# Block 2 of a four-block network: weight pieces between the context's tiles, softmax shifts from the sums alone

## The chip, the cores and the metric

The kernel runs on one core of a Trainium2 chip. The metric is device time in microseconds of one execution; lower is better. The engines are named as in the profile: PE (matrix products and transposes), DVE (VectorE), ACT (ScalarE), POOL (GpSimd) and SP (which issues most DMAs). They run side by side, each through its own queue in order, and wait for one another through semaphores.

## The reference

Four transformer blocks (L0 to L3) work one after the other on `x` of shape 4x1024x288, with a context of 4x64 rows. The change is in block L2, which quantizes its attention to 8 bits with one scale per tensor. Cut to what matters:

```python
def _fake_quant(x, n_bits, always_zero=False):
    ...
    xq = jnp.clip(_ste_round(x / delta) + zp, 0.0, levels)
    return (xq - zp) * delta

def _quant_attention(x, ctx, Wq, Wk, Wv, Wo, bo):
    q, k, v = ...                       # 16 heads of 18
    q = _fake_quant(q, NBITS)
    k = _fake_quant(k, NBITS)
    v = _fake_quant(v, NBITS)
    scores = jnp.einsum('bhqd,bhkd->bhqk', q, k) * scale
    probs = jax.nn.softmax(scores, axis=-1)
    probs = _fake_quant(probs, SMBITS, always_zero=True)   # one scale: max(probs) / 255
    out = jnp.einsum('bhqk,bhkd->bhqd', probs, v)
    return out.transpose(0, 2, 1, 3).reshape(bsz, sq, D) @ Wo + bo

n1 = _ln(h, ln1_g, ln1_b)
h = h + _quant_attention(n1, n1, Wq1, Wk1, Wv1, Wo1, bo1)                       # self-attention
h = h + _quant_attention(_ln(h, ln2_g, ln2_b), encoder_hidden_states, ...)      # context
n3 = _ln(h, ln3_g, ln3_b)
a, gate = jnp.split(n3 @ Wff1 + bff1, 2, axis=-1)
h = h + a * jax.nn.gelu(gate, approximate=False) @ Wff2 + bff2
```

The scale of the probabilities is their maximum over all rows and heads. So no probability can be rounded before all of them have been seen once.

## The kernel before

A tile is 128 rows of `x`; there are 32, eight to each of the four batch entries. The 16 heads are padded from 18 to 32 columns and stand in four groups (`g`) of four heads, so that a group fills 128 partitions after a transpose. A framework plans the order within each engine's queue from the order in which the code is traced, priorities and modelled times; `tc.issue_after(i)` puts what it encloses behind instruction `i` on `i`'s engine. In `fq_tail`, SP alone keeps the order of the code. A tile of a pool that takes over memory waits for the last reader of what lay there.

Block L2 runs through these stages:

- The projections write `raw`, queries, keys and values of all tiles, to DRAM, and their extremes give the scales `q` (`super().global_params`, with one reduction over the partitions on POOL).
- **First pass** (`fq_passes`, first half). `fetch` brings columns of `raw` into one of three buffers `in`; `fq_levels` and `place` round them and put them into padded tiles `pads`; `operands` or `both` transposes these on PE and ACT copies them to `qk` (L3180). For batch entry 0 the keys are made by DVE, and the queries by the generator `first_queries` on POOL. Then for each group, tile and pair of heads: scores on PE (`scores_pair`, L3842), exponentials with row sums on ACT (L3244), and the largest exponential of each row on DVE (L3251). While one batch entry is scored, `levels` prepares the next on POOL.
- **Hand-over.** `largest` turns sums and maxima into the largest probability, `prob_params` makes the scale `pd` of it over all partitions by way of PE. Each row then gets a shift, minus the logarithm of sum times `pd`: `y = sums * pd`, its Ln and one correction step (`log_shifts`), split into three bf16 parts. `add_shift` puts the parts into three of the unused rows of each head in `qk`'s queries (D to D+2, through `spad` on POOL, a transpose and an addition on DVE); the keys hold ones in these rows, so that the score's product adds the shift.
- **Second pass** (`attend_levels`). For half a batch entry (512 queries), group and tile of keys `kt`: scores from `kz`, the keys of a group spread with zeros by SP's DMAs (`spread`); exponentials (L3891) that come out as levels, rounding on DVE (L3897) and products with the values (L3865). `beside_half` does one step of other work at each `kt`: it adds the shifts of the next half, and projects and normalizes the last one.
- **Context** (`fq_tail`). `largest(t)` makes a tile's query levels (L819, L820, L3545), transposes them (L3551), writes them to `qb` in DRAM (L3555), scores them (L3558) and takes maxima (L3565); POOL does every second tile from the fourth on. `total(n, qT)` sums the exponentials of four tiles (L3576 to L3607). After the first four, `load_halves` loads the feed-forward weight `w1`: a large load and six pieces of 384 columns through two buffers `w3`, each cast and subtracted on DVE (L2661, L2662), and then `w2` and the biases. Afterwards shifts are made on POOL (`parts_of`) from the logarithm of the sums alone, and the scale's logarithm enters the exponential as a bias `lp[:, 2:3]`.

Of the kernel before, what the change touches and what calls it, by code (L numbers as in the profile page):

```python
# [37 lines left out]
P = 128  # L38
# [1142 lines left out]
class Fast(Net):  # L1181
# [65 lines left out]
    def prob_params(self, pool, r, name):  # L1247

        nc = self.nc
        s = pool.tile([P, 1], F32, name=f"{name}s")  # L1250
        nc.vector.tensor_reduce(s, r, AX.X, ALU.max)
        d = pool.tile([P, 1], F32, name=f"{name}d")
        nc.vector.tensor_scalar(
            d, self.largest_of(pool, s, name), 1.0 / 255.0, None, ALU.mult
        )
        return d
# [1393 lines left out]
    def load_halves(self, pool, scratch, w, n, name, step):  # L2650
# [5 lines left out]
        for c0 in range(0, n, step):  # L2656
            m = min(step, n - c0)
            cols = slice(c0, c0 + m)
            y = scratch.tile([P, step], F32, tag="w3", name="w3", bufs=2)[:, :m]
            nc.sync.dma_start(y, w[2 * P :, cols])  # L2660
            nc.vector.tensor_copy(c[:, cols], y)  # L2661
            nc.vector.tensor_tensor(  # L2662
                c[64:, cols], y[64:], c[64:, cols].bitcast(F32), ALU.subtract
            )
        return t, c
# [248 lines left out]
    def fq_attn(self, w, ctxT, beside):  # L2914
# [10 lines left out]
        with ExitStack() as es:  # L2925
# [145 lines left out]
            self.watch_range(-0.5, 255.5, q["zp"], "zext")  # L3071

# [7 lines left out]
    def fq_passes(self, w, q, step, raw, rawq, qmx, qmn, side, aside):  # L3080

        tc, nc = self.tc, self.nc
        with ExitStack() as es:
# [7 lines left out]
            nc.gpsimd.memset(v[:, :, C:], 0.0)  # L3091

            kzs = [gp.tile([P, 2, S], BF16, name="kz0")]
# [12 lines left out]
            top = tp.tile([P, NT, H], F32, name="top")  # L3106
            sums = tp.tile([P, NT, H], F32, name="sums")
            r = tp.tile([P, NT, H], F32, name="rs")
            tmx = tp.tile([P, B], F32, name="tmx")
            with (  # L3110
# [7 lines left out]
                for pd in pads:  # L3118
                    nc.gpsimd.memset(pd, 0.0)
                    nc.gpsimd.memset(pd[:, 1, :, D : D + 3], 1.0)  # L3120

                def fetch(b, n, j0, m):

                    y = ld.tile([P, 3 * C], F32, tag="in", name="in")
# [4 lines left out]
                def place(b, n, j, y, eng):  # L3129
# [6 lines left out]
                    eng.tensor_scalar(dst, src, q["top"][:, n : n + 1], None, ALU.min)  # L3136

                def first_queries():

                    for j0 in range(0, NTB, 3):  # L3140
# [65 lines left out]

                fq0 = first_queries()
                next(fq0)
                for j0 in range(0, NTB, 3):
                    m = min(3, NTB - j0)  # L3210
                    y = fetch(0, 1, j0, m)
# [5 lines left out]
                operands(0, 0, 0, 1)  # L3217
                nc.gpsimd.memset(kzs[0], 0.0)
                for sp in spads:
                    nc.gpsimd.memset(sp, 0.0)  # L3220
                spare = iter(())
                for b in range(B):
                    ahead = levels(b + 1) if b + 1 < B else first_values()
                    for g in range(NG):
                        for qt in range(NTB):
# [3 lines left out]
                            with tc.issue_after(self.last) if n or b else nullcontext():  # L3229
                                if b == 0 and g == 0 and qt + 1 < NTB:  # L3230
# [8 lines left out]
                            for pr in range(2):  # L3239
# [3 lines left out]
                                for j, sc in enumerate(scs):  # L3243
                                    nc.scalar.activation(  # L3244
# [5 lines left out]
                                    )  # L3250
                                nc.vector.tensor_reduce(top[:, t, h0 : h0 + 2], e, AX.X, ALU.max)  # L3251
                            if n in (2, 3):
                                next(spare, None)
                    if b + 1 < B:
# [6 lines left out]
                    spare = largest(b)  # L3261
                for _ in spare:
                    pass
            es.enter_context(self.psum("f1o"))
            pd = self.prob_params(gp, tmx, "pd")
            rt = gp.tile([P, 1], F32, name="rstep")
            nc.vector.reciprocal(rt, step)
            parts = gp.tile([P, 3, NT * H], BF16, name="parts")
            flat = lambda ap: ap.rearrange("p t h -> p (t h)")
            y = flat(sums)  # L3270
            z, u = (tp.tile([P, NT * H], F32, name=k) for k in ("lsz", "lsu"))
            nc.vector.tensor_scalar(y, y, pd, None, ALU.mult)
            nc.scalar.activation(z, y, AF.Ln)

            def log_shifts(c0, c1):

                yc, zc, uc = (ap[:, c0:c1] for ap in (y, z, u))
                nc.scalar.activation(uc, zc, AF.Exp, scale=-1.0)
                nc.vector.tensor_tensor(uc, uc, yc, ALU.mult)
                nc.vector.tensor_scalar(uc, uc, -1.0, 1.0, ALU.mult, ALU.add)  # L3280
                nc.vector.tensor_tensor(uc, uc, zc, ALU.subtract)
                nc.vector.tensor_scalar(uc, uc, rt, None, ALU.mult)
                for k in range(3):
                    nc.vector.tensor_copy(parts[:, k, c0:c1], uc)
                    if k < 2:
                        nc.vector.tensor_tensor(uc, uc, parts[:, k, c0:c1], ALU.subtract)

            def shifts(b, hf):
                for j in range(hf * 4, hf * 4 + 4):
                    t = b * NTB + j  # L3290
                    self.add_shift(
                        qk[:, b, 0, :, j * P : (j + 1) * P], spads[j % 2], parts, t
                    )
                    yield

            with tops:
                log_shifts(0, NTB * H)
                for _ in shifts(0, 0):
                    pass
# [706 lines left out]
```

## Time and profile before

| what | value |
|---|---|
| median of 3 runs | 4738.31 us (4733.14 to 4739.08) |
| the profiled execution | 4733.92 us, its span 4732.1 us |
| busy PE, DVE, ACT, POOL | 4196.1, 3077.9, 2999.1, 1193.8 us |
| mean granted PE clock | 0.88 |
| first pass, first to last reduction of L3251 | 1734.06 to 2304.84 us |
| second pass, exponentials L3891 | 2323.22 to 2824.25 us |
| context, first level to `pds` | 2858.25 to 2981.60 us |

The times of the stages are microseconds from the start of the span. A matmul's end is modelled, so PE's busy time is no measure of its rate. The chain of waits that the profile follows back from the end names, in each stretch, what the following work waited for.

### The profile page before, as it was taken

To read this page: it belongs to the slowest core of one execution; us is meant where nothing else is said; L and a number is where in the kernel's file an instruction comes from. 1 tells how busy PE (TensorE), PEld (TensorE's weight loads), DVE (VectorE), ACT (ScalarE), POOL (GpSimd) and SP (SyncE) were. 2 spreads that over 40 slices of the span, in tenths; PEclk is the share of its full clock that TensorE was granted. 3 is DMA by queue.
4 is the path that set the end of the run, shared out by engine and by line. 5 is a ranking of instruction groups with operands and counts; after the bars stand their busy time and mean duration, and the time that the engine had idled before them with its cause. 6 is when DMAs were issued, how large, how long until landed. Compare 5 with 4: busy or idle time off the path is not lost. (4 is left out here: it accounts for less than half of the span.)

```text
span 4732.1 us, 62855 instructions
## 1 busy us (share of the span) xinstructions
PE 4196.1 (89%) x22841; PEld 1741.1 (37%) x22841; DVE 3077.9 (65%) x6914; ACT 2999.1 (63%) x4277; POOL 1193.8 (25%) x1797
## 2 busy tenths in 40 slices
PE   4999998889988889999789986899998999998887
PEld 2223323455566531111123333455552233223444
DVE  8355445786644779999888986544346446446886
ACT  2776776566753259999799973322215776775665
POOL 2001001333210567440013343210101000002453
PEclk9999999889999875555589997899998999998898
DMA  3000002110000321000001014001001000001000
GB/s 88 2 6 22 9 11 54 56 42 6 13 13 17 113 92 42 27 18 0 14 21 29 26 29 144 21 21 19 0 19 26 2 10 26 7 12 39 15 18 19
DMA packets 138592, 135.92 MB, mean 29 GB/s; under 512 B 69404, under 2 KB 116124, under 8 KB 136736
## 3 DMA queue, kind: packets, MB, share of 16 engines
q1 hardware_dynamic: 137072, 128.13, 9.2%
q0 software_dynamic: 1200, 3.69, 0.4%
q8 instruction: 181, 2.97, 0.3%
q14 instruction: 139, 1.14, 0.1%
HBM read 79.92 MB, written 43.47 MB: 26 GB/s over the span
## 5 line engine op out<-in xcount | busy, mean ns | idle before, releaser
L2196 ACT ACTIVATE e<-ps 128x1024 f32<-128x1024 f32 x1024 | 992.6, 1021 | 412.0 <-PE ps L2186 404.6
L2186 PE MATMUL ps<-qT,kT 32*128 32x512 f32 x4096 | 624.3, 647 | 2.0 <-DVE sext L2108 2.0
L3251 DVE TENSOR_REDUCE top<-e 128x2 f32<-128x2048 f32 x256 | 563.5, 2273 | 15.4 <-ACT e L3244 15.2
L2142 PE MATMUL ps<-e,v 128*32 128x512 f32 x4096 | 553.9, 612 | 9.0 <-DVE oT L2153 9.0
L3842 PE MATMUL ps<-qk 32*128 32x512 bf16 x1024 | 500.7, 604 | 40.3 <-ACT e L3244 38.6
L3244 ACT ACTIVATE e<-ps 128x1024 f32<-128x1024 f32 x512 | 521.6, 1190 | 6.6 <-PE ps L3842 3.1
L3891 ACT ACTIVATE e<-ps 128x1024 f32<-128x1024 f32 x512 | 477.1, 1080 | 33.3 <-PE ps L3882 18.5
L3897 DVE TENSOR_SCALAR eb<-e 128x2048 bf16<-128x2048 f32 x256 | 323.8, 1270 | 48.4 <-ACT e L3891 47.3
L1921 POOL TENSOR_TENSOR x<-x,y 128x288 f32<-128x288 f32 x188 | 149.1, 805 | 812.2 <-DVE y L1919 484.8
L2693 PE MATMUL psf<-hT,w 128*128 128x512 f32 x576 | 271.9, 594 | 0.7 <-ACT hT L2684 0.6
L2186 PEld LDWEIGHTS ps<-qT,kT 32*128 32x128 f32 x4096 | 184.8, 185 | 202.1 <-issue 130.3
L3882 PE MATMUL ps<-qk,kz 64*128 64x512 bf16 x1024 | 216.7, 423 | 32.3 <-ACT e L3891 27.4
L2142 PEld LDWEIGHTS ps<-e,v 128*32 128x32 f32 x4096 | 81.3, 108 | 402.7 <-issue 345.0
L3842 PEld LDWEIGHTS <-qk 32*128 32x128 bf16 x1024 | 53.1, 99 | 465.6 <-issue 464.6
L3758 ACT ACTIVATE gl<-psf,bf 128x512 f32<-128x512 f32 x72 | 49.3, 685 | 243.6 <-PE psf L2694 235.0
L2038 POOL TENSOR_TENSOR v<-y,wv1b 128x288 f32<-128x288 f32 x64 | 51.0, 802 | 565.1 <-DVE y L2035 565.1
L3244 ACT ACTIVATION_READ_ACCUMULATOR e<-ps 128x1 f32 x512 | 192.1, 375 | 0.0
L1535 POOL TENSOR_TENSOR h<-h,g 128x288 f32<-128x288 f32 x108 | 88.0, 815 | 355.5 <-ACT h L1532 355.5
L279 PEld LDWEIGHTS <-qT 98*128 98x128 bf16 (+2 forms) x1344 | 130.1, 103 | 127.4 <-ACT qT L1437 38.9
L2153 DVE COPY oT<-ps 128x512 f32<-128x512 f32 x64 | 44.1, 689 | 202.0 <-PE ps L2142 202.0
L3762 DVE SCALAR_TENSOR_TENSOR u<-psf,bf,gl 128x512 f32<-128x512 f32 x72 | 53.6, 748 | 153.0 <-PE psf L2694 152.8
L3773 PE MATMUL psf<-w,u 128*128 128x288 f32 x576 | 147.0, 410 | 0.0
(579 smaller groups left out, 7970.4 us busy)
## 6 DMA issues: line engine op xcount, KB each, us to landing
raw<-y SPq DMA_DIRECT2D x32, 432.0 KB
in<-raw SPq DMA_DIRECT2D x30, 432.0 KB
kz<-qk SPq DMA_DIRECT2D x128, 64.0 KB
wn<-in_L_wfc SPq DMA_DIRECT2D x12, 432.0 KB
x<-in_x SPq DMA_DIRECT2D x4, 1152.0 KB
vvo<-vt SPq DMA_DIRECT2D x16, 288.0 KB
vo<-vvo SPq DMA_DIRECT2D x4, 1152.0 KB
qn<-rawq SPq DMA_DIRECT2D x4, 1152.0 KB
```

Source lines behind the costliest of these rows:

```text
L1921: eng.tensor_tensor(self.x[:, t, :], self.x[:, t, :], y, ALU.add)
L2142: nc.tensor.matmul(acc[i * HP : (i + 1) * HP, :], lhsT=st["v"][:, kt, h * (D + 1) : h * (D + 1) + HP], rhs=es_[i // 2][:, i % 2, :], start ...
L2186: nc.tensor.matmul(pss[i // 2][:, i % 2, :], lhsT=self.row_tile(kT, i)[:, kt * P : (kt + 1) * P], rhs=self.row_tile(qT, i)[:, qh * 512 : ( ...
L2196: nc.scalar.activation(e, ps, AF.Exp, scale=SCALE)
L2693: nc.tensor.matmul(o, lhsT=a[:, c, :], rhs=b[:, c, :], start=(c == 0), stop=False)
L3244: nc.scalar.activation(e[:, j, :].rearrange("p (a n) -> p a n", a=2), sc, AF.Exp, scale=rstep, accum_out=sums[:, t, h0 + j : h0 + j + 1],)
L3251: nc.vector.tensor_reduce(top[:, t, h0 : h0 + 2], e, AX.X, ALU.max)
L3773: nc.tensor.matmul(ps[:, :C], lhsT=us[f][:, j * P : (j + 1) * P], rhs=w2[:, f, :], start=(f == 0), stop=(f == nf - 1),)
L3842: self.last = self.nc.tensor.matmul(ps[:, c, :], lhsT=self.row_tile(qT, i)[:, g, qt * P : (qt + 1) * P], rhs=self.row_tile(kT, i)[:, g, c ...
L3882: nc.tensor.matmul(pss[i][:, n, :], lhsT=kz[rows, i, kt * P : (kt + 1) * P], rhs=qT[rows, g, qh * 512 : (qh + 1) * 512], start=True, stop= ...
L3891: nc.scalar.activation(e[:, 2 * n : 2 * n + 2, :], ps, AF.Exp, scale=step)
L3897: nc.vector.tensor_scalar(eb, e, MAGIC, MAGIC, ALU.add, ALU.subtract)
```

## The change

Five things change in L2:

- Query tile 0 is fetched alone and made by DVE ahead of the keys, and the last two keys are fetched into a buffer of the exponentials. The transposes of query tile 1 come after the first pair of heads. The memsets of `v`, `kzs` and `spads` move from ahead of the pass to its tile 8, on POOL; range checks move behind the start.
- The shifts are made from the sums alone, on POOL, in the manner of the context stage (`log_parts`). For the first half of batch entry 0 they don't hold the scale; for all other rows the scale's part `lp[:, 2:3]` is added before the split.
- For that first half the scale's part enters as a bias of the exponential in group 0, and for groups 1 to 3 through three more rows (D+3 to D+5, six rows of ones in the keys), which one addition fills (`lps`).
- In the second pass's first half `beside_half` does that addition and the scaling of `wo`, and starts the shifts of the next half ten steps later.
- In the context stage DVE makes the levels of all tiles, and the six pieces of `w1` are loaded one per tile by a generator, after `w2` and the biases have been issued.

The diff, cut to its core:

```diff
-    def load_halves(self, pool, scratch, w, n, name, step):
+    def halves_pieces(self, pool, scratch, w, n, name, step):
 ...
+        def pieces():
+            for c0 in range(0, n, step):
 ...
+                nc.sync.dma_start(y, w[2 * P :, cols])
+                nc.vector.tensor_copy(c[:, cols], y)
+                nc.vector.tensor_tensor(
+                    c[64:, cols], y[64:], c[64:, cols].bitcast(F32), ALU.subtract
+                )
+                yield
+
+        return (t, c), pieces()
 ...
+            def log_parts(lz, lu, c0, c1, one):
+
+                yc, zc, uc = (a[:, c0:c1] for a in (flat(sums), lz, lu))
+                eng = nc.gpsimd
+                eng.tensor_tensor(uc, uc, yc, ALU.mult)
+                eng.tensor_scalar(uc, uc, -1.0, one, ALU.mult, ALU.add)
+                eng.tensor_tensor(uc, uc, zc, ALU.subtract)
+                eng.tensor_scalar(uc, uc, rt, None, ALU.mult)
+                for k in range(3):
+                    i = eng.tensor_copy(parts[:, k, c0:c1], uc)
+                    if k < 2:
+                        eng.tensor_tensor(uc, uc, parts[:, k, c0:c1], ALU.subtract)
+                return i.ins
 ...
-                    nc.gpsimd.memset(pd[:, 1, :, D : D + 3], 1.0)
+                    nc.gpsimd.memset(pd[:, 1, :, D : D + 6], 1.0)
 ...
-                fq0 = first_queries()
-                next(fq0)
+                y = fetch(0, 0, 0, 1)
+                self.fq_levels(y[:, 0, :], q, 0)
+                place(0, 0, 0, y[:, 0, :], nc.vector)
+                operands(0, 0, 0, 1)
+                fq0 = first_queries()
                 for j0 in range(0, NTB, 3):
                     m = min(3, NTB - j0)
-                    y = fetch(0, 1, j0, m)
+                    y = None
+                    if j0 == 6:
+                        y = ep.tile([P, 2, S], F32, tag="e", name="e").rearrange("p a n -> p (a n)")
+                    y = fetch(0, 1, j0, m, y)
 ...
-                operands(0, 0, 0, 1)
-                nc.gpsimd.memset(kzs[0], 0.0)
-                for sp in spads:
-                    nc.gpsimd.memset(sp, 0.0)
+                next(fq0)
+                self.watch_range(-0.5, 255.5, q["zp"], "zext")
 ...
+                                if b == 0 and n == 0 and pr == 0:
+                                    operands(0, 0, 1, 1)
 ...
+                            if b == 0 and n == NTB:
+                                with tc.issue_after(self.placed):
+                                    nc.gpsimd.memset(v[:, :, C:], 0.0)
+                                    for t in (*kzs, *spads):
+                                        nc.gpsimd.memset(t, 0.0)
 ...
+                lz, lu = (
+                    ld.tile([P, 3 * C], F32, tag="in", name="in")[:, : NT * H] for _ in range(2)
+                )
+                with tc.issue_after(ended):
+                    nc.scalar.activation(lz, flat(sums), AF.Ln)
+                    ended = nc.scalar.activation(lu, lz, AF.Exp, scale=-1.0).ins
+                with tc.issue_after(ended):
+                    nc.scalar.activation(lp[:, 0:1], rt, AF.Ln)
+                log_parts(lz, lu, 0, NTB * H // 2, 1.0)
                 for _ in spare:
                     pass
+                pd = self.prob_params(gp, tmx, "pd")
+                with tc.issue_after(self.reduced):
+                    for _ in shifts(0, 0):
+                        pass
+                nc.scalar.activation(lp[:, 0:1], pd, AF.Ln)
+                nc.scalar.activation(lp[:, 1:2], lp[:, 0:1], AF.Exp, scale=-1.0)
 ...
+                done = nc.vector.tensor_tensor(lp[:, 2:3], lp[:, 1:2], lp[:, 0:1], ALU.subtract).ins
+                with tc.issue_after(self.copied):
 ...
+                for c0, c1 in ((NTB * H // 2, NTB * H), (NTB * H, NT * H)):
+                    with tc.issue_after(self.copied):
+                        self.copied = log_parts(lz, lu, c0, c1, lp[:, 3:4])
 ...
-            nc.vector.tensor_scalar(y, y, pd, None, ALU.mult)
-            nc.scalar.activation(z, y, AF.Ln)
 ...
+                if not n:
+                    yield
+                    with tc.issue_after(self.levelled):
+                        nc.vector.tensor_scalar(
+                            qk[:, 0, 0, 1:, :512], qk[:, 0, 0, 1:, :512], lps[:, 2:3], None, ALU.add
+                        )
 ...
-                    eng = nc.gpsimd if t > 2 and t % 2 else nc.vector
-                    self.fq_levels(qn[:, t, :], q, 0, eng)
-                    eng.tensor_scalar(
+                    self.fq_levels(qn[:, t, :], q, 0)
+                    nc.vector.tensor_scalar(
 ...
                         running = [t for t in running if next(t, running) is not running]
+                        next(pieces, None)
 ...
-                        w1 = self.load_halves(wp, qp, w["Wff13"], 2 * FF, "w1", 384)
+                        w1, pieces = self.halves_pieces(wp, qp, w["Wff13"], 2 * FF, "w1", 384)
 ...
-                    nc.scalar.activation(e[:, 2 * n : 2 * n + 2, :], ps, AF.Exp, scale=step)
+                    nc.scalar.activation(
 ...
+                        **({} if g or bias is None else {"bias": bias}),
+                    )
```

## The prediction

> **What bounds the kernel now.** I read the page first, then the chain of waits, then the timeline engine by engine at the four places that the diff touches: the start of block 2's first pass, the hand-over to its second pass, the start of that pass, and the context's tiles. All lie in order in time and the second block after them waits for them, so what a stage gives back ends the program earlier. The page's groups for the first pass:
>
> ```profile
> L3251 DVE TENSOR_REDUCE top<-e 128x2 f32<-128x2048 f32 x256 | 563.5, 2273 | 15.4 <-ACT e L3244 15.2
> L3244 ACT ACTIVATE e<-ps 128x1024 f32<-128x1024 f32 x512 | 521.6, 1190 | 6.6 <-PE ps L3842 3.1
> ```
>
> VectorE's 256 reductions fill 563.5 us and were idle only 15.4, of which 11.06 lie before the first. So the pass ends a fixed time after its first reduction. The timeline at its start (start, duration, engine, line; idle before it and its releaser in brackets):
>
> ```profile
> 1721.39 0.49 POOL L819 TENSOR_SCALAR in<-in,gqrd 128x288 f32<-128x288 f32 x1 [7.77 <-ACT qk L3180]
> ...
> 1728.77 1.02 ACT L3244 ACTIVATE e<-ps 128x1024 f32<-128x1024 f32 x1 [1.12 <-PE ps L3842]
> ...
> 1731.78 0.61 PE L3175 MATMUL ps<-idb,pads 128*128 128x128 bf16 x4 [3.04 <-POOL pads L3136]
> ...
> 1732.90 1.03 ACT L3244 ACTIVATE e<-ps 128x1024 f32<-128x1024 f32 x1
> ...
> 1734.06 15.80 DVE L3251 TENSOR_REDUCE top<-e 128x2 f32<-128x2048 f32 x7 [11.06 <-ACT e L3244]
> ```
>
> The first query tile comes from POOL, late; then PE stands 3 us in front of the second tile's transposes with half of the first pair of scores still to do. The hand-over between the passes:
>
> ```profile
> 2298.18 6.66 DVE L3251 TENSOR_REDUCE top<-e 128x2 f32<-128x2048 f32 x3
> ...
> 2307.32 0.15 DVE L1251 TENSOR_REDUCE pds<-tmx 128x1 f32<-128x4 f32 x1
> ...
> 2309.88 1.28 ACT L3273 ACT_TABLE_LOAD   x1 [11.60 <-DVE pv L3304]
> ...
> 2323.22 3.77 ACT L3891 ACTIVATE e<-ps 128x1024 f32<-128x1024 f32 x4 [9.38 <-PE ps L3882]
> ```
>
> From the reduction `pds` to the second pass's first exponential go 15.9 us, since the logarithm of sums times scale waits for the scale. The context stage already takes the logarithms apart, and its same stretch shows the price of the new order:
>
> ```profile
> 2981.60 0.16 DVE L1251 TENSOR_REDUCE pds<-tmx 128x1 f32<-128x8 f32 x1
> ...
> 2987.12 4.73 ACT L3699 ACTIVATE ec<-ps,lp 128x512 f32<-128x512 f32 x8 [1.50 <-POOL lsu L3642]
> ```
>
> There it is 5.5 us. Last, the stall among the context's tiles:
>
> ```profile
> 2876.97 28.27 SPq L2660 DMA_DIRECT2D w<-in_L_Wff  x6
> ...
> 2906.45 8.97 SPq L3555 DMA_DIRECT2D qb<-qT  x10
> ...
> 2913.61 1.07 ACT L3554 COPY qT<-ps 128x512 bf16<-128x512 bf16 x2 [14.96 <-DMA qb<-qT]
> ...
> 2914.26 1.03 PE L3558 MATMUL ps<-kbd,qT 128*128 128x256 bf16 x4 [15.17 <-ACT qT L3554]
> ```
>
> SP, in order, holds six weight pieces on two buffers; from the third on each waits for VectorE's cast. Ten writes of `qb` queue behind them, ScalarE's copy waits for its buffer, and PE stands 15.17 us.
>
> **The change part by part**
>
> *Start of the first pass.* VectorE gets three operations on 128x288 for query tile 0, about 0.29 each (two of L3136 took 0.65): +0.9; five range checks and a reciprocal at about 0.07 leave: -0.4. The last keys go to an `e` tile, so their fetch no longer waits for a buffer released at 1717.53: VectorE's 1.37 us wait goes, and POOL no longer runs beside its last placements (1.38 for two instead of 0.65). The last placement, which ended at 1722.99, ends near 1721.8. From there the trace needs 1.71 us to the end of the keys' copy and 1.07 from score to exponential: first exponential at 1724.7, the second at once since the transposes for tile 1 now stand behind the first pair. First reduction 1726.8 against 1734.06: **-7.3** (-4.5 if the `e` tile comes free late and the keys land as before). POOL makes tile 1 in 2.75 us (0.49+1.25+1.0) from 1721.4, and later ones faster than VectorE's 4.4 us per tile (563.5/128), so it isn't next.
>
> *Hand-over.* The two range reductions over `rs` (0.59 each in sequence) stood between the product and `tmx`; they move behind the scale, so `pds` comes 1.2 earlier, 2306.1; plus 5.5 as in the context stage: first exponential 2311.6 instead of 2323.22, **-11.6**. What must be ready by then: ScalarE ends its exponentials at 2298.28; two table loads, Ln and Exp took 3.75 for 448 columns in the context stage: 2302.1. POOL's nine operations on 64 columns took 3.36 there and two copies 0.43: 2305.9. Transposes (1.7) and four additions on VectorE at 0.34 end by 2309.5. Slack 2 us. If the additions sit in front of the scale's chain on VectorE they cost 1.4; if the planner runs POOL's part after the scale, 3.8 more; bounds -6 to -12.
>
> *Start of the second pass, added work.* One addition on 128x1536 bf16 (the 512 took 0.34 in sequence: about 1), the scale into `wo` 0.82, range check 1.7: 3.5 us on VectorE over the first three steps. A step takes 1.83 us of ScalarE and 1.14 of VectorE, so 0.7 is free in each and two `e` buffers give another step: +1. POOL's ten operations on one to three columns have no row here; the nearest are 0.12 (L3532) and 0.32 (64 columns): 1.2 to 3.2 us, and the addition behind them waits at worst 1 us. Then parts for 64 and 384 columns, 3.4 and about 9 us, on POOL, needed only at step 13 or later. `wq2`'s load on SP waited for the old tiles' last reader (2318.74 after the last cast); now that reader is POOL, at about 2326 in old time, and the keys for group 1, needed at 2326, could stand behind it: 0 to +3. Together **+1** (0 to +5).
>
> *Context's tiles.* With one piece per tile, `qb`'s eighth write stands behind piece 2 alone. If the first cast still runs near 2896, that write lands some 2.5 us later (one piece took 2.47), so 13 of the 15.17 go. Added on VectorE: levels and placement of 15 tiles that POOL did. At the rows' means (0.522+0.520+0.426) 22 us, without POOL beside it 0.29 each, 13 us. The 17 tiles it has already lose that contention: -17x2x0.23 = -8. How much is on the path: from 2866 to 2889 VectorE is the chain itself and ran levels ahead of ready reductions, afterwards it is idle 4.1 of each 10.63 us for four tiles (L3596 at 2939.98 and 2950.61), which also hides most of the pieces' 5.7 us. I put +2: **-11** (-15 to -3, the latter with ten more us in the early stretch).
>
> *At nothing.* The memsets of `v`, `kz`, `spad` (5 us) go to tile 8 of the first pass, where POOL is busy 34.8 of 50 us; uncovered they delay tiles needed four tiles (18 us) later. More ones in `pads`, `kz1` in another pool: no instruction on the path.
>
> Sum: -7.3 - 11.6 + 1 - 11 = -28.9. The profiled execution took 4733.92 (span 4732.1 and 1.8 around it), so 4705.0; the median of the runs is 4.4 higher, so 4738.3 - 28.9 = **4709**.
>
> **Rivals**
>
> *The stall only moves.* The pieces land behind 2304 KB and now also 1296 KB; if VectorE's queue has the casts as late as before, SP blocks at piece 2 and at each pair again. For it: the casts came at 2899.5 though the DMA had gone quiet at 2885. Then the stage gives nothing: -18, **4720**.
>
> *POOL and VectorE hold each other up.* In the second pass's first 15 us POOL computes parts beside eight levels L3897. Their row over the pass is 1192/1226/1826 ns: 0.6 us lost at the worst, 8x0.6 = 5 us if nothing hides it: **4714**. Against: from 2500 to 2700 POOL is busy 29 to 48% and ScalarE still 97%. The Trainium skill, SBUF — State Buffer, "Who interferes with whom", says that VectorE in a two-port mode and GpSimd exclude each other for a whole instruction, which speaks against this placement; by that rule the time would be this rival's 4714.
>
> *VectorE becomes the bound of the context stage* (the slower side). It was busy 73.4 us there:
>
> ```profile
> 2858.00:2899.00 41.00, 26.97 (x160) 12.97 (x160) 33.62 (x59) 16.41 (x25) 33.90 (x37) 0.74 0.59 229
> 2899.00:2914.00 15.00, 0.09 (x2) 0.00 (x0) 5.77 (x13) 0.39 (x1) 0.00 (x0) 0.64 0.71 199
> 2914.00:2982.00 68.00, 59.13 (x353) 26.46 (x353) 33.97 (x56) 42.99 (x61) 11.17 (x19) 0.90 0.17 42
> ```
>
> (after the length: busy time of PE, its weight loads, VectorE, ScalarE, POOL.) If 22 us of levels and six waits of 2.47 for pieces all lie on the path, +36.8, and the stall stays, the sum is +19, **4757**. It passes the kernel before by over 0.2% once 27 of the 36.8 are on the path. Against: 55% busy and 4.1 us free per four tiles.
>
> **How the numbers follow.** The forecast has 0.52 (its own range 4703 to 4722), POOL against VectorE 0.13, the moved stall 0.18, VectorE as bound 0.11, gains and losses that cancel 0.06. 0.2% is 9.5 us, about what a measurement tells from no change. Faster 0.83, same 0.06, slower 0.11. The range reaches from the best terms (-35, and 6 us of spread among the runs) to the worst that still gains: 4697 to 4728.
>
> **What would show it.** First reduction L3251 about 2 us after the first exponential instead of 5.3; `pds` to first exponential near 5.5 us; PE's longest wait before L3558 under 4 us; from the context's first level to its `pds` about 112 us instead of 123.4. Wrong if VectorE shows waits for DMA `w` among the tiles, or if ScalarE's idle time before the second pass's exponentials stays above 5 us.

## The result and the profile after

The changed kernel takes 4721.8 us (median of 10 runs, 4719.7 to 4725.8) against 4738.7 us of the kernel before on the same chip (10 runs): 0.9968, 95% interval 0.996 to 0.9977, so 16.9 us less. The forecast was 4709. The profiled execution took 4721.5 (span 4719.7).

By stages, each from the profile's own times in us. The first row starts at `gqd`, the scale of the projections, which is the first step that both kernels reach alike:

| stage | before | after | difference | predicted |
|---|---|---|---|---|
| `gqd` to first reduction of the first pass | 20.4 | 15.9 | -4.5 | -7.3 |
| first reduction to end of the last | 570.8 | 571.1 | +0.3 | 0 |
| to `pds`, and on to the first exponential | 2.5 + 15.9 | 1.6 + 6.6 | -10.2 | -11.6 |
| second pass, first to last exponential's end | 501.0 | 504.3 | +3.3 | +1 |
| on to the context's first level | 34.0 | 34.1 | +0.1 | 0 |
| first level to the context's `pds` | 123.3 | 113.2 | -10.1 | -11 |
| sum | 1267.9 | 1246.8 | -21.1 | -28.9 |

Outside these stages the instructions of the two kernels are the same, yet the profile after reaches `gqd` 5.3 us later (1719.0 against 1713.7) and takes 3.4 us longer from the context's `pds` to the end. What is known of that stands at the end of the part on the prediction.

The groups of the first pass in the kernel after:

```profile
L3299 DVE TENSOR_REDUCE top<-e 128x2 f32<-128x2048 f32 x256 | 563.5, 2276 | 12.7 <-ACT e L3292 12.5
L3292 ACT ACTIVATE e<-ps 128x1024 f32<-128x1024 f32 x512 | 522.0, 1192 | 5.5 <-PE ps L3906 2.0
```

The pass itself is unchanged: 563.5 us of reductions. Their idle time fell only from 15.4 to 12.7. The timeline at its start says why:

```profile
1726.78 0.99 POOL L819 TENSOR_SCALAR in<-in,gqrd 128x288 f32<-128x288 f32 x2 [7.82 <-DVE bad L1275]
...
1731.33 0.60 PE L3212 MATMUL ps<-idb,pads 128*128 128x128 bf16 x4 [3.83 <-POOL pads L3171]
...
1732.69 1.02 ACT L3292 ACTIVATE e<-ps 128x1024 f32<-128x1024 f32 x1
...
1734.85 2.29 DVE L3299 TENSOR_REDUCE top<-e 128x2 f32<-128x2048 f32 x1 [8.11 <-ACT e L3292]
```

The keys were ready as early as forecast (scores began at 1727.11). But PE's transposes of query tile 1 stand in the middle of the first scores and wait for POOL, whose first operation again started 7.8 us after the reduction over the partitions. A second wait lies hidden in that stretch. POOL's queue stands in a wait for a semaphore for 7.76 us, until 1726.22:

```profile
1718.55 0.40 POOL L793 PARTITION_ALL_REDUCE gqr<-gqs  x1 [18.37 <-DVE gqs L791]
...
1722.57 3.02 SPq L3161 DMA_DIRECT2D in<-raw  x3
```

What it waits for is the landing of the first of these three fetches, that of query tiles 1 to 3. SP could issue it only at 1722.57, when VectorE had placed query tile 0 out of the same buffer. In the kernel before, the fetch of POOL's first tiles had been issued by 1591. The hand-over:

```profile
2307.58 0.16 DVE L1251 TENSOR_REDUCE pds<-tmx 128x1 f32<-128x4 f32 x1
...
2312.39 0.68 DVE L1269 TENSOR_REDUCE wr<-rs 128x1 f32<-128x512 f32 x1
...
2312.99 0.41 DVE L2600 TENSOR_TENSOR qk<-qk,ps 128x512 bf16<-128x512 bf16 x1
...
2314.19 2.12 ACT L3955 ACTIVATE e<-ps,lp 128x1024 f32<-128x1024 f32 x2 [2.83 <-DVE wr L1272]
```

From `pds` to the exponential it is 6.6 us instead of 15.9. The first half of the range check stands ahead of the fourth addition into `qk`; the check itself (`wr`), which the row names as what released the exponential, isn't among what that reads. The context's tiles:

```profile
2881.28 0.52 SPq L3616 DMA_DIRECT2D qb<-qT  x1
...
2893.16 0.35 DVE L2663 CAST w1h<-w 128x384 fp32r<-128x384 f32 x1
...
2894.40 0.33 SPq L2662 DMA_DIRECT2D w<-in_L_Wff  x1
...
2897.49 1.07 ACT L3615 COPY qT<-ps 128x512 bf16<-128x512 bf16 x2 [11.51 <-DMA qb<-qT]
...
2898.13 1.04 PE L3619 MATMUL ps<-kbd,qT 128*128 128x256 bf16 x4 [11.72 <-ACT qT L3615]
```

The stall is still there, 11.72 us of 15.17. SP stands from 2881.8 to 2894.4 in front of the third piece, whose buffer comes free when the first piece has been cast and subtracted (2893.16 to 2894.38); between 2886.7 and 2893.2 VectorE ran 23 level operations in a row. Yet the stage is 10.1 us shorter: the stall is 3.5 us shorter and begins 34 us after the first level instead of 41.

### The profile page after: what moved, and what is told of

Same layout as the page of the kernel before. It is cut to its first block, busy times and chain, and to the rows that moved or that the text cites. A ratio compares the mean times of both kernels' runs of the same rounds, so it can differ in the third digit from the quotient of the medians.

```text
span 4719.7 us, 62858 instructions
## 1 busy us (share of the span) xinstructions
PE 4200.0 (89%) x22841; PEld 1745.3 (37%) x22841; DVE 3080.4 (65%) x6948; ACT 3004.9 (64%) x4281; POOL 1173.8 (25%) x1786
## 4 chain that ended last, share of the span: by engine, by line
PE 34%; DVE 15%; ACT 8%; POOL 3%; issue 3%; DMA 0%; ACTq 0%; DVEq 0%; POOLq 0%; SPq 0%
PE psf L2704 5%; PE ps L2186 5%; PE ps L2142 5%; DVE top L3299 4%; PE ps L3906 4%; ACT e L3955 3%; PE ps L279 3%; PE psf L3837 3%; ACT e L3292 3%; DVE eb L3967 2%; PE ps L2054 1%; PE ps L3946 1%; POOL x L1925 1%; PE psf L2705 1%; PE ps L3929 1%
## 5 line engine op out<-in xcount | busy, mean ns | idle before, releaser
L3299 DVE TENSOR_REDUCE top<-e 128x2 f32<-128x2048 f32 x256 | 563.5, 2276 | 12.7 <-ACT e L3292 12.5
L3955 ACT ACTIVATE e<-ps 128x1024 f32<-128x1024 f32 x496 | 462.9, 1071 | 24.9 <-DVE eb L3967 12.4
L3967 DVE TENSOR_SCALAR eb<-e 128x2048 bf16<-128x2048 f32 x256 | 325.4, 1276 | 46.8 <-ACT e L3955 45.5
```

Source lines behind the costliest of these rows:

```text
L3955: nc.scalar.activation(e[:, 2 * n : 2 * n + 2, :], ps, AF.Exp, scale=step, **({} if g or bias is None else {"bias": bias}),)
L3967: self.levelled = nc.vector.tensor_scalar(eb, e, MAGIC, MAGIC, ALU.add, ALU.subtract).ins
```

## The experiments

Ratios are to the kernel before, run beside it. The times of one kernel scatter by 5 to 25 us, so where a few microseconds matter the stage times of the profiles decide.

**The context stage: pieces or levels.** `e1_pieces` is the kernel before with `halves_pieces` and one `next(pieces, None)` per tile, and nothing else:

> Kernel before, with the six weight pieces alone taken one per tile; levels still alternate between POOL and VectorE. Theory of the prediction (the pieces' queue on SP makes the stall): PE's longest wait before the scores of the context's tiles falls from 15.17 us to about 2, first level to pds from 123.4 to about 110.5 us, time 4738.7 - 13 = 4726. Theory from the traces (SP still blocks at the third piece, since the first cast stands late in VectorE's queue; the gain of the change came from the levels): PE's longest wait 11 to 13 us, first level to pds about 120 us, time 4735.

`e2_levels` is the kernel before with

```diff
-                    eng = nc.gpsimd if t > 2 and t % 2 else nc.vector
-                    self.fq_levels(qn[:, t, :], q, 0, eng)
+                    self.fq_levels(qn[:, t, :], q, 0)
```

and the placement on VectorE too:

> Kernel before, with all levels of the context's tiles on VectorE and nothing else changed; the six pieces still stand together on SP. Theory of the prediction (the levels cost VectorE about 2 us on the path): the 15 us wait stays, first level to pds 123.4 to 126 us, time 4738.7 + 2 = 4741. Theory from the traces (the levels alone bring the stage 7 us forward ahead of the stall): start of the 15 us wait some 34 us after the first level instead of 41, wait still about 15 us, first level to pds about 116.5 us, time 4732.

Measured: `e1_pieces` 4724.3 us, ratio 0.9977 (0.9965 to 0.9989), the stage 113.5 us; `e2_levels` 4731.4 us, 0.9987 (0.9976 to 0.9998), the stage 118.3 us. PE's longest waits, `e1_pieces` first:

```profile
2904.15 1.03 PE L3569 MATMUL ps<-kbd,qT 128*128 128x256 bf16 x4 [5.05 <-ACT qT L3565]
```

```profile
2913.02 1.03 PE L3557 MATMUL ps<-kbd,qT 128*128 128x256 bf16 x4 [17.64 <-ACT qT L3553]
```

So my reading of the trace after was wrong for the pieces: alone they bring 9.8 us (123.3 to 113.5), close to the prediction's 13. The levels alone bring 5.0, and the prediction had them as a loss of 2. But together they bring 10.1, not 14.8: with all levels on VectorE the stage reaches SP's block 7 us sooner and then waits for the same late cast. The profiles bear this out: the first cast comes 41.3 us after the first level in `e1_pieces` and 40.6 in the changed kernel, PE's long wait ends 4.7 to 5.0 us behind it in both, and from there to `pds` it is 67 to 68 us, as in the kernel before and in `e2_levels`.

**Where the rest of the stall comes from.** `e3_poolq` issues the six pieces from POOL's queue, `e5_order` holds levels back, `e9_cast5` adds a place for the casts:

```diff
-                    self.fq_levels(qn[:, t, :], q, 0)
+                    with tc.issue_after(reds[t - 4]) if t > 3 else nullcontext():   # e5_order
+                        self.fq_levels(qn[:, t, :], q, 0)
```

> Changed kernel, with the six pieces of w1 issued from POOL's queue instead of SP's. Theory from the traces (what is left of the stall is SP blocked at the third piece until the first cast has run): no wait of PE over 4 us before the scores of the tiles, first level to pds about 103 us instead of 113.2, time 4722 - 10 = 4712. Rival (behind SP's block VectorE or the landing of qb is next at once, so the stall only changes its name): first level to pds 110 us or more, time 4719 to 4722.

> Changed kernel, with VectorE's levels of the context's tile t held behind the reduction of tile t-4. Theory (VectorE runs two dozen levels in one go ahead of the first piece's cast, so SP, which waits for that cast, holds the writes of qb): the first cast runs about 34 us after the stage's first level instead of 40.6, PE's longest wait before the scores is 5 to 6 us instead of 11.7, first level to pds about 107 us instead of 113.2, time 4721 - 6 = 4715. Rival (the piece lands late behind the large loads, so that the cast can't run earlier): VectorE waits for w before the first cast, wait and stage as in the changed kernel, 113 us, 4721.

> As the run before, and the levels of tile t held behind the cast of the piece that was issued with tile t-5, so that the first cast stands behind the ninth reduction. Theory (the late cast is the whole of the stall): PE's longest wait under 4 us, first level to pds about 103 us, time 4721 - 10 = 4711. Rival (VectorE now waits for the pieces to land, and the reductions behind it in its queue wait with it): waits of VectorE for w of 5 us or more, first level to pds 108 us or more, time 4716 or more.

| run | median, us | ratio | first level to `pds` | PE's longest wait behind the first tile |
|---|---|---|---|---|
| `e3_poolq` | 4714.3 | 0.9957 (0.9942 to 0.9972) | 110.8 | 7.16 |
| `e5_order` | 4709.4 | 0.994 (0.9927 to 0.9954) | 109.0 | 4.17 |
| `e9_cast5` | 4719.4 | 0.9962 (0.9948 to 0.9975) | 118.6 | 10.17 |

`e5_order` confirms the theory, though the stage is 109.0 us and not the expected 107: the first cast runs 33.8 us after the first level (40.6 in the changed kernel), and waited 0.84 us for its piece, so it could hardly be earlier:

```profile
2883.55 0.36 DVE L2663 CAST w1h<-w 128x384 fp32r<-128x384 f32 x1 [0.84 <-DMA w<-in_L_Wff]
...
2888.15 1.04 PE L3622 MATMUL ps<-kbd,qT 128*128 128x256 bf16 x4 [4.17 <-ACT qT L3618]
```

The stage gives 4.2 us, while the runs took some 12 less than the changed kernel's, and the profiled one was the slowest of the five (4715.3). What gave the rest no trace here shows.

`e9_cast5` shows the other side. Put behind the ninth reduction instead of the twelfth, the same cast stops the whole of VectorE until the piece lands, and PE waits for VectorE's tiles:

```profile
2883.76 0.36 DVE L2663 CAST w1h<-w 128x384 fp32r<-128x384 f32 x1 [7.85 <-DMA w<-in_L_Wff]
...
2886.13 0.61 PE L3619 MATMUL ps<-idb,pads 128*128 128x128 bf16 x4 [10.17 <-DVE pads L3613]
```

In `e3_poolq` SP is free, and VectorE's order is at fault twice. The first piece is now issued before the tiles begin, so its cast stands ahead of the first level and waits:

```profile
2859.37 0.36 DVE L2663 CAST w1h<-w 128x384 fp32r<-128x384 f32 x1 [3.48 <-DMA w<-in_L_Wff]
```

and later 12 us of levels run in one go ahead of a reduction that was ready for the last 7 of them. The first level comes 4.9 us later, so the profile gains nothing on the changed kernel, although the timed runs gained some 7 us. The profiled execution took 4722.7 us, 8.4 above the median; what was faster in the timed ones no trace here shows, so this run's time stays open.

**The start of the first pass.** `e4_start` holds tile 1's transposes and copy back; `e6_tile1` also makes tile 1 on VectorE:

```diff
-                                    operands(0, 0, 1, 1)
+                                    operands(0, 0, 1, 1, ended)  # behind self.last on PE, behind ended on ACT
...
-                y = fetch(0, 0, 0, 1)
+                y0 = fetch(0, 0, 0, 2)                            # e6_tile1
...
-                next(fq0)
+                self.fq_levels(y0[:, 1, :], q, 0)
+                place(0, 0, 1, y0[:, 1, :], nc.vector)
```

> Changed kernel, with the transposes of query tile 1 held behind the first pair of scores on PE and their copy behind the first pair's exponentials on ScalarE. Theory from the traces (these two stand ahead of the second score and the first exponential and wait for POOL's tile): scale gqd to first reduction 12 to 13 us instead of 15.8, and the pass ends as much earlier, time 4722 - 3 = 4719. Rival (tile 1 comes from POOL so late that the reductions wait for it in any case): the first reduction is early, but VectorE is idle about 3 us before the third, and the time stays at 4722.

> As e4_start, and query tile 1 made by VectorE too, behind the keys, so that POOL begins with tile 2. Theory (POOL's first operation starts some 8 us after the partition reduction whatever its place, so tile 1 from POOL is what the third reduction waits for): gqd to first reduction about 12.5 us, no idle time over 1 us before the next three reductions, first to last reduction about 571.5 us, time 4721 - 3.5 = 4717. Rival (tile 2 is late in the same way): first to last reduction 574 us or more, time 4720 to 4722.

`e4_start`: 4720.4 us, 0.9968 (0.9956 to 0.998); `e6_tile1`: 4722.8 us, 0.9974 (0.9964 to 0.9984). The first reduction came at `gqd` + 11.9 in both, as the theory had it, 3.9 us sooner than in the changed kernel. And both lost it again: first to last reduction took 575.8 and 574.5 us instead of 571.1. In `e4_start` VectorE stood idle for 2.27 us before the second reduction, since tile 1's transposes, which wait for POOL, now stand ahead of the second pair's scores, and for 2.17 before the thirteenth. In `e6_tile1` only the latter wait is left, 30 us after the first reduction:

```profile
1751.18 0.61 PE L3213 MATMUL ps<-idb,pads 128*128 128x128 bf16 x4 [3.99 <-POOL pads L3171]
...
1754.94 2.29 DVE L3302 TENSOR_REDUCE top<-e 128x2 f32<-128x2048 f32 x1 [3.29 <-ACT e L3295]
```

PE waits there for the last query tile, which POOL placed behind levels of the next batch entry.

**The start of the second pass.** Taken index by index, 2.2 of the 3.3 us of the pass are lost in its first 48 exponentials: from the first to the 49th it takes 45.5 us before and 47.7 after (47.1 to 48.7 in the repaired kernels below). Profiles of one code differ less than that: 44.7 to 45.5 in the three whose pass is that of the kernel before, 47.6 to 48.5 in the six whose pass is that of the kernel after. The other 1.0 us lies further on, where `before` and `e1_pieces`, with the same pass, are 1.1 apart; it is left open. `e8_nolate` leaves out POOL's late work, `e7_nobias` the bias, `e11_neither` both:

```diff
-                for c0, c1 in ((NTB * H // 2, NTB * H), (NTB * H, NT * H)):
+                for c0, c1 in ((NTB * H // 2, NTB * H),):                # e8_nolate, e11_neither
...
-  self.attend_levels(..., rstep, None if n else lp[:, 2:3], late, aside)
+  self.attend_levels(..., rstep, None, late, aside)                     # e7_nobias, e11_neither
```

> Changed kernel without the logarithm's parts of the last 384 columns on POOL; the shifts of all halves take those of the first 128 columns, so the values of the later halves differ from the reference. Theory (POOL's work and VectorE's levels hold each other up at the start of the second pass): first to last exponential of the pass 501 to 502.5 us instead of 504.3, and no idle time of ScalarE over 1 us in the pass's first 30 us. Rival (the extra 3 us are the exponentials with a bias): still 503.5 to 504.5 us.

> Changed kernel without the bias of the exponentials of group 0 in the second pass's first half; the scale is left out of those rows, so their values differ from the reference. Theory (a bias per partition costs 0.07 to 0.1 us per exponential, 16 of them): the first 16 exponentials of the pass take about 15 us instead of 16.5 from the first start to the seventeenth, and the first 48 take 46.2 instead of 47.7. Rival (the first exponentials are slow because PE and VectorE are late for them): the first 16 still take 16 us or more.

> Changed kernel with both of the last two taken away: no bias in group 0 of the second pass's first half, and no logarithm's parts of the last 384 columns on POOL; values differ from the reference in both places. Theory (each alone hides behind the other: without the bias ScalarE only reaches VectorE's late levels sooner, without POOL's work the biased exponentials are the limit): from the first to the 49th exponential about 45 us, as in the kernel before, instead of 47.7 (47.9 without the bias alone, 46.9 without the parts alone). Rival (the addition to qk, the scale into wo and the other added work on VectorE are the rest): 46 us or more.

| from the first exponential to the | before | after | `e8_nolate` | `e7_nobias` | `e11_neither` |
|---|---|---|---|---|---|
| 17th | 15.0 | 16.5 | 16.0 | 15.3 | 14.8 |
| 33rd | 30.3 | 33.0 | 32.0 | 33.2 | 30.3 |
| 49th | 45.5 | 47.7 | 46.9 | 47.9 | 45.5 |

One run of each, with 4719.6, 4713.7 and 4716.5 us; their times tell nothing at this size. The table does: without the bias the start is faster and the gain is gone by the 33rd; without POOL's work 0.8 is left at the 49th; without both the whole 2.2 is back, within the 0.8 by which profiles of the old start differ. Two causes overlap, and either hides most of the other. My expectation for `e8_nolate` (the pass 2 to 3 us shorter) failed for that reason: 504.1 against 504.3. The bias costs ScalarE 0.07 to 0.09 us per exponential. The rows of line L3955 in the kernel after (least, median and most ns):

```profile
L3955 ACT ACTIVATE e<-ps x496: 1015/1042/1287, 2330.7 to 2817.5; 128x1024 f32<-128x1024 f32 x166
...
L3955 ACT ACTIVATE e<-ps,lp x16: 1107/1116/1160, 2314.2 to 2329.7; 128x1024 f32<-128x1024 f32 x16
```

The Trainium skill, ScalarE: Activation LUTs, "What ACT_TABLE_LOAD costs", gives about 93 ns for each operand of one value per partition; the least of these rows differ by 92 ns, their medians by 74. The other cause is a memory wait. The timeline after:

```profile
2333.53 0.50 POOL L3131 CAST parts<-in 128x384 bf16<-128x384 f32 x1
...
2334.06 0.69 DVE L3937 COPY oT<-ps 128x512 f32<-128x512 f32 x1 [1.96 <-POOL parts L3131]
...
2335.99 1.94 ACT L3955 ACTIVATE e<-ps 128x1024 f32<-128x1024 f32 x2 [1.49 <-DVE eb L3967]
```

The first copy into `oT` starts 0.03 us after POOL's last part ends. `oT` is made of none of POOL's results, so what ties it to them is memory: the tile takes over that of the buffers `in`, which hold the logarithms, and POOL is now their last reader. (No view shows addresses; the profiles show only that the wait ends with POOL's last part.) The levels stand behind that copy on VectorE, and ScalarE behind the levels. The copy came 26.5 us after `pds` in the kernel after, 26.8 in `e7_nobias` and 26.6 in `e10_all`, each time 0.03 us behind the last part; in `e8_nolate`, where POOL was done long before, it waited 0.97 us for PE. The sizes fit the table: 16 biased exponentials at 0.07 to 0.09 us are 1.2 to 1.5, and ScalarE's wait behind the copy is 1.49 us instead of 0.50 in `e8_nolate`, so 1.0. In `e7_nobias` that wait grew to 3.04, which is where the gain of the missing bias went.

**The repairs together.** `e10_all` has `e5_order`'s levels, `e6_tile1`'s start with POOL's levels of the next batch entry held behind the last query tile, and the range check behind the last addition:

```diff
-                with tc.issue_after(done):
+                with tc.issue_after(added):
                     self.watch_range(self.R_MIN, self.R_MAX, flat(r), "wr")
```

> Changed kernel with three repairs: levels of context tile t behind the reduction of tile t-4 (as in e5_order); query tile 1 on VectorE (as in e6_tile1) and POOL's levels of the next batch entry behind the last query tile; the range check of rs behind the last addition of the hand-over. Theory (the 3.8 us that e6_tile1 lost again are the last query tile, which POOL made behind other levels; the check held back the fourth addition): gqd to first reduction 12 us and first to last reduction 571.2 us, pds to first exponential 6.0 us instead of 6.6, first level to pds 109 us; together 4 + 0.6 + 4.2 = 8.8 us less than the changed kernel, time 4712. Rival (POOL, 2.74 us per tile from 8 us after the reduction on, is the limit of the first eight tiles in any order): first to last reduction 574 us or more, time 4716.

4705.0 us (4703.0 to 4708.0), ratio 0.9933 (0.992 to 0.9947). First reduction at `gqd` + 11.9 and 571.3 us for the pass: this time the 4 us were kept, so the order on POOL was the cause, not its speed. `pds` to first exponential 6.2 us, first level to `pds` 107.9. The wait of the copy into `oT` was longer, 2.93 us. Stage by stage the profile is 8.7 us below that of the changed kernel, as expected (8.8); the two profiles are 18.6 us apart and the medians 16.8, so about half of the gain lies outside these stages, where the instructions are the same. `e12_early` takes two of POOL's steps ahead of the scale:

```diff
+            def log_sums(lz, lu, c0, c1):
+                yc, zc, uc = (a[:, c0:c1] for a in (flat(sums), lz, lu))
+                nc.gpsimd.tensor_tensor(uc, uc, yc, ALU.mult)
+                return nc.gpsimd.tensor_tensor(uc, uc, zc, ALU.add).ins
...
+                with tc.issue_after(self.copied):
+                    self.copied = log_sums(lz, lu, NTB * H // 2, NT * H)
```

> As e10_all, and the two steps of the logarithm's correction that don't need the scale (product with the sums, addition of the logarithm) done on POOL ahead of the scale for all rows. Theory (the first copy into oT lies on memory of the logarithms and waits in VectorE's queue for POOL's last reader, which ended 26.5 us after pds in three profiles, with the next levels behind it): the last parts end about 23.5 us after pds, the copy into oT waits for PE alone, and the first 48 exponentials of the pass take 46.5 to 47 us instead of 48.7; time 4705 - 2 = 4703. Rival (VectorE's levels beside POOL are the limit, not the copy): the copy comes sooner, but the first 48 still take 48 us or more, time 4705.

4698.8 us (4692.4 to 4700.6), ratio 0.9918 (0.9904 to 0.9931), the best version here. The last part ended 23.1 us after `pds`, and the copy waits for PE alone:

```profile
2320.07 1.38 POOL L3135 CAST parts<-in 128x384 bf16<-128x384 f32 x1
...
2323.61 0.69 DVE L3956 COPY oT<-ps 128x512 f32<-128x512 f32 x1 [0.97 <-PE ps L3948]
```

The first 48 exponentials took 47.1 us instead of 48.7, a little over the expected 46.5 to 47; `pds` to the first exponential took 6.9 us, 0.7 more than in `e10_all`, which no run takes apart. Not all of the gain on `e10_all` is this repair: the plan of the queues came out differently elsewhere too. The second pass is 7.6 us shorter than in `e10_all`, of which 1.6 lie in the first 48 exponentials and 4.2 in the last 63, and the context's stage, with the same edits, is 3.3 longer (111.2).

## Why the prediction was right in sign and 13 us off

The direction held and each of the four terms has the right sign; two were mis-sized, and one came out nearly right by other steps than I gave.

- *Start of the first pass, -7.3: measured -4.2.* The keys came as early as worked out. The step that failed is "the second at once since the transposes for tile 1 now stand behind the first pair": the code says so, the planned order doesn't, and PE stood 3.83 us in it. So the sign "first reduction about 2 us after the first exponential" came true (2.15) while the term failed, since the first exponential itself was held, to `gqd` + 13.7 instead of 11. POOL began where I had it, in part by luck: I had not seen that the fetch of tile 1 now waits for tile 0's buffer, and that fetch landed only 0.56 us before POOL's start. It made two tiles at once, so that tile 1 was placed 4.5 us after the start and not 2.75; "so it isn't next" failed with that. `e4_start` got the early start and lost it to tile 1 from POOL, `e6_tile1` to the last tile; only `e10_all`, with POOL's order set as well, kept it (583.1 us from `gqd` to the end of the pass, against 587.0).
- *Hand-over, -11.6: measured -10.2.* Mechanism right. `pds` came 0.9 us earlier relative to the last reduction and not 1.2, and the context's 5.5 us was 6.6 here. The range check ahead of the fourth addition is 0.4 of that, which `e10_all` got back; the other 0.7 no run takes apart.
- *Second pass, +1: measured +3.3.* The term for the bias was missing, although the row of `ec<-ps,lp` was in view. The wait for memory was named, for `wq2` and the keys behind it; it came on the copy into `oT`, in VectorE's queue. So the step "needed only at step 13 or later" failed: POOL's parts were waited for behind the eighth levels. They also took longer than I had them, 5.3 us for 64 columns and 14.0 for 384 (with two copies for `spad` between) instead of 3.4 and about 9. The rival that POOL and VectorE hold each other up gave 5 us at the worst; levels took up to 2.01 us beside POOL after, as that rule of the Trainium skill (SBUF — State Buffer, "Who interferes with whom") would have it, and 1.21 in the same place in `e8_nolate`. But with the bias and the wait for memory the 2.2 us are accounted for; what the slower levels add is not seen.
- *Context's tiles, -11: measured -10.1, by other steps.* The pieces' -13 was nearly right alone (-9.8 in `e1_pieces`). The levels' +2 had the wrong sign: alone they brought -5.0 (`e2_levels`), since the chain of levels at the stage's start reaches the stall 7 us sooner. I had a credit of 8 us there against 13 of added work, and mixed in it the duration of an operation beside POOL (0.52) with the time from one start to the next without (0.29); the durations are 0.52 and 0.36. Whether VectorE's quicker levels or the loss of POOL's slower tiles (2.8 us each, by the rows' means) brought the 7 us, no run separates. What also failed is adding the two: they meet at one cast. So the sign in "what would show it" held for the stage (112 forecast, 113.2 measured), while the wait of PE, forecast under 4 us, was 11.72: the total came out nearly right because the levels gained where the pieces did not. VectorE's waits for `w`, which I had named as a sign of being wrong, are there with 1.60 and 0.78 us, behind the first cast.
- *The rival "the stall only moves"* gave 4720 and described the stall better than my forecast did: the casts are late in VectorE's queue, and SP blocks at piece 2. It was wrong that the stage then gives nothing. *VectorE as bound of the context stage* didn't come in this kernel; `e9_cast5`, with 118.6 us, shows the form in which it would have.

The terms make 21.1 us in the two profiles, the runs 16.9 with an interval of about 11 to 19. The difference lies outside these stages. In 14 profiles, whose instructions are the same there, the time to `gqd` went from 1712.2 to 1723.1 us and that from the context's `pds` to the end from 1741.5 to 1755.7. The latter goes with PE's granted clock: its mean over this stage was 0.946 in the fastest and 0.937 to 0.939 in the five slowest. Before's profile has 0.941, after's 0.937; the three kernels without the change of the passes range from 0.940 to 0.946, the eleven with it from 0.937 to 0.944. Whether the change itself makes the clock after it a little lower, or the runs fell so, isn't settled.

## What to carry to other kernels

When two edits of one stage release the same wait, look for the one instruction at which both end (here a cast in VectorE's queue): their gains don't add. Where that instruction stands is then the next thing to change (4.2 us of the stage in `e5_order`). A buffer freed later by a slower engine is paid for by whoever is given its memory next, and that can be a tile with no other tie to it. An order that the code states in passing isn't an order: read the queues, and pin what matters on every engine that the step passes through.

## What the runs showed of the hardware

- POOL's first operation after the reduction over the partitions came 7.7 to 8.7 us after it in all 14 profiles, while the releaser named for it was ACT's copy or DVE's `in`, `bad`, `zext` or `rstep`. In the kernel before, `e1_pieces` and `e2_levels` nothing that it reads was late: the tiles had been fetched, and the scale `gqrd` was ready 7.2 to 7.5 us before the start. So there it looks like a cost of its own and not a wait, though no run took the reduction away. In the other eleven its queue also stood in the wait for a fetch until 0.15 to 1.48 us before the start, so there the two lie on top of each other. The Trainium skill, GPSIMD Engine Reference, "Instruction dispatch", has some 6 us for the first call of a freshly loaded kernel, with no instruction visible; the rows here show more.
- A level operation on 128x288 in the context's tiles took 0.36 us on VectorE without POOL beside it (mean of 32), against 0.52 before (mean of 17), where POOL did every second tile: moving work to the busier engine made the stage faster, by 5.0 us in `e2_levels`.
- The same instructions after block 2 took up to 14.3 us more or less from one profile to the next, with the granted clock.
